# One product out of several in an adapter and feed-forward kernel: float32 replaced by float32r on operands split into exact parts

## The chip, the cores and the metric

The kernel runs on one core of a Trainium2 chip. The metric is the device time of one execution in microseconds (us). The core's engines appear in the profile as PE (TensorE, matrix products; PEld is its loading of weights), DVE (VectorE), ACT (ScalarE), POOL (GpSimd) and SP (the engine that here issues nearly all DMAs). A "q" behind a name (SPq) means the engine's sequencer. PSUM is the memory that PE writes; here it is eight buffers that all stages share.

## The reference

There are 8 batches of 256 tokens, x of shape (8, 256, 1024). Each batch b names one of 8 adapters by itok[b]. What is computed:

```
Bx  = x[b] @ B[id].T            # rank 16
c   = Bx @ A[id].T              # back to 1024
g   = fp8(c / in_scale) @ gate_w.T        # 2752 columns, weights are fp8 values
u   = fp8(c / in_scale) @ up_w.T
h   = silu(g * scales) * u * scales
out = x + (fp8(h / in_scale) @ down_w.T) * scales
```

The roundings to fp8 make it matter that c is as exact as float32: an error in c can move a value to its neighbour in fp8.

## The kernel before

The tokens are 2048 columns in four blocks t of 512 columns, two batches each. x is held transposed: 128 partitions by 8 slices k by 512 columns. The work goes in this order, and PE's order is the order of the program, since `multiply` (L470) pins every matmul to it.

- Block 0: `two_times_b(0)` (L500) forms Bx, `two_times_a(0)` (L531) forms c, and c is rounded to fp8 (xg) by `round_to` (L524), half on DVE (L527), half on ACT (L529). PE is kept busy by products of zeros ("warm", `pass_time`) until the data are there.
- `gate_up(c, 0)` (L581) for the first five chunks c of the hidden dimension (128 of 2752 columns each): 16 fp8 products of 512 columns into two PSUM buffers y (gate and up), then ACT's silu (g, L610) and DVE's product (hid, L611). In the fifth of them, twelve products in, `two_times_b(1)` is put between.
- Block 1: `two_times_a(1)`, then `gate_up(c, 1)` for the same five chunks. The first of these takes its slices of xg in turns of two, as they come. In the fourth, eight products in, `four_times_b()` (L552) forms Bx of the four batches of blocks 2 and 3; after it, `four_times_a` (L560) makes c for the first half of the 1024 rows, and in the middle of the fifth for the second half.
- Then `gate_up` of all other chunks and blocks, and the down projection (yd), each result with x added going out by DVE (o, L696) and SP.

The products with B and A are small and are packed by row or column quarters of PE's array. Each has float32 operands. For Bx, the 32 columns of B that a product takes (`b[:, at : at + 32]`) hold the 16 of one slice k and 16 of a neighbour or padding; the result is 32 rows in a quarter of PSUM's partitions. For block 1, A is stored in a zeroed tile so that only 16 of the quarter's 32 rows count (`load_a_two`, L370, row `32 * (2 * g + j) + R * j`); for blocks 2 and 3 only 16 rows of each quarter are used (L565). A group of c is four PSUM buffers, one for each row quarter q, and each buffer holds two slices k of 256 columns. In blocks 0 and 1 a product has 128 columns, because the two halves of Bx are placed in both orders (`other`) in the tile bm by copies of DVE and ACT (L517); in blocks 2 and 3 it has 256 columns, and bm is one copy of DVE (L557).

The loads stand on SP's queue in this order: x of block 0 with B and A of batches 0 and 1, the weights of the first five chunks, B of block 1 (two loads b), x of block 1 in two pieces (slices 0 to 6, 1792 KB; slice 7, 256 KB), A of block 1 (four loads of 32 KB), then x of block 2, two loads of b_four, x of block 3, two more, four loads of a_four (64 KB each), w_dt, and the weights of later chunks as their buffers come free. Each DMA of the queue waits for the semaphore of the DMA eight places before it.

The tiles hid0 to hid20 (128 by 2048 bytes) hold the rounded hidden values; chunk c writes hid[c], so most of them are empty in the first 60 us.

Of the kernel before, what the change touches and what calls it, by code (L numbers as in the profile page):

```python
# [8 lines left out]

F32 = mybir.dt.float32  # L10
BF16 = mybir.dt.bfloat16
FP8 = mybir.dt.float8e4
U16 = mybir.dt.uint16
I32 = mybir.dt.int32
AF = mybir.ActivationFunctionType
ALU = mybir.AluOpType
AX = mybir.AxisListType

P = 128
T = 2048  # L20
SEQ = 256
NB = 8
H = 1024
I = 2752
R = 16
NH = H // P
NI = (I + P - 1) // P
# [5 lines left out]
NFIRST = 5  # L33

BROW = NH * R + 8
# [15 lines left out]
def high(ap):  # L51

    return ap.bitcast(BF16)[..., 1::2]

# [229 lines left out]
def adaln_ffn(  # L284
# [13 lines left out]
    nc = tc.nc  # L298
    const = ctx.enter_context(tc.tile_pool(name="const", bufs=1))
# [22 lines left out]
    kept = ctx.enter_context(tc.tile_pool(name="kept", bufs=1))  # L322
    wpool = ctx.enter_context(tc.tile_pool(name="w", bufs=5))
    outs = ctx.enter_context(tc.tile_pool(name="outs", bufs=3))
    hid = [kept.tile([P, T], FP8, name=f"hid{c}") for c in range(NI - 1)]


    hid_tail = kept.tile([P, 2, TB], BF16, name="hid_tail")
# [8 lines left out]
    with ExitStack() as fast:  # L337
        acts = fast.enter_context(tc.tile_pool(name="acts", bufs=1))
        lora = fast.enter_context(tc.tile_pool(name="lora", bufs=1))
# [12 lines left out]
        b_two = [lora.tile([P, 2 * BROW + R], F32, name=f"b{t}") for t in range(2)]  # L352
        a_two = [lora.tile([P, H // 2], F32, name=f"a{t}") for t in range(2)]

        b_four = lora.tile([P, 4 * BROW + R], F32, name="b_four")
        a_four = lora.tile([P, H], F32, name="a_four")
        nc.gpsimd.memset(a_two[0], 0.0)
        nc.vector.memset(a_two[1], 0.0)
        for b, n in ((b_two[0], 2), (b_two[1], 2), (b_four, 4)):
            nc.vector.memset(b[:, n * BROW :], 0.0)  # L360

# [8 lines left out]
        def load_a_two(t, j, adapter, queue=nc.sync):  # L370
            for g in range(2):
                row = 32 * (2 * g + j) + R * j
                queue.dma_start(  # L373
                    out=a_two[t][row : row + R],
                    in_=a8[bass.ds(adapter * 2 * R + g * R, R), :],
                )

        def load_x(t, k):
            piece, first = x_of(x4, t, k)
            ks = slice(first, first + piece.shape[1])  # L380
            nc.sync.dma_start(out=xs[t][:, ks, :], in_=piece)
# [25 lines left out]
        adapters = [adapter_of(2 + q, nc.sync) for q in range(6)]  # L407
        for j in range(2):
            load_b(b_two[1], j, adapters[j], nc.sync)
        for k in (0, 7):  # L410
            load_x(1, k)
        for j in range(2):
            load_a_two(1, j, adapters.pop(0))

        for t in (2, 3):
            load_x(t, 0)
            for q in (2 * t - 4, 2 * t - 3):
                load_b(b_four, q, adapters[q], nc.sync)
        for q in range(4):
            nc.sync.dma_start(  # L420
                out=a_four[32 * q : 32 * q + R], in_=aT[bass.ds(adapters[q] * R, R), :]
            )


        sc = b_two[0][:, NH * R : BROW]
        inv = const.tile([P, 6], F32, name="inv")
# [43 lines left out]
        def multiply(*args, **kwargs):  # L470
            tc.keep_in_program_order(nc.tensor.matmul(*args, **kwargs))  # L471
# [12 lines left out]
        def times_b(bx, b, n, quads, between=None):  # L484


            for k in range(NH):
                for q, (i, row, t, cols) in enumerate(quads):
                    at = i * BROW + k * R - row
                    multiply(  # L490
                        bx[q][32 * q : 32 * (q + 1)],
                        lhsT=b[:, at : at + 32],
                        rhs=xs[t][:, k, cols],
                        start=(k == 0),
                        stop=(k == NH - 1),
                    )
                if between:
                    between(k)

        def two_times_b(t, between=None):  # L500


            n = SEQ // 2
            quads = [
                (j, R * j, t, slice(at, at + n))
                for half in range(2)
                for j in range(2)
                for at in (j * SEQ + half * n,)
            ]
            bx = [psum.tile([P, n], F32, tag="ps", name=f"bx{half}") for half in range(2)]  # L510
            times_b([bx[q // 2] for q in range(4)], b_two[t], n, quads, between)
            bm = lora.tile([P, 2, n], F32, tag="bm2", name="bm2", bufs=2)
            for other in range(2):
                for half, copy in enumerate((nc.vector.tensor_copy, nc.scalar.copy)):
                    to = half ^ other
                    tc.keep_in_program_order(
                        copy(  # L517
                            bm[64 * to : 64 * (to + 1), other],
                            bx[half][64 * half : 64 * (half + 1)],
                        )  # L520
                    )
            return bm

        def round_to(to, c, engine):  # L524
            scale = inv[:, GATE_IN : GATE_IN + 1]
# [2 lines left out]
            else:  # L528
                nc.scalar.activation(to, c, AF.Copy, scale=scale, saturate=False)  # L529

        def two_times_a(t, bm):  # L531


            n = SEQ // 2
            for part in range(2):
                cs = [psum.tile([P, 2, SEQ], F32, tag="ps", name=f"c{q}") for q in range(4)]
                for other, i in product(range(2), range(2)):
                    for q in range(4):
                        rows = slice(32 * q, 32 * (q + 1))
                        multiply(  # L540
                            cs[q][:, i, bass.ts(q // 2 ^ other, n)],
                            lhsT=a_two[t][rows, bass.ts(2 * part + i, P)],
                            rhs=bm[rows, other],
                            start=True,
                            stop=True,
                        )
                for q in range(4):
                    k = KS * part + 2 * (q // 2)
                    to = xg[t][:, k : k + 2, bass.ts(q % 2, SEQ)]
                    round_to(to, cs[q], nc.vector if q % 2 else nc.scalar)  # L550

        def four_times_b():  # L552
            quads = [(q, 0, 2 + q // 2, bass.ts(q % 2, SEQ)) for q in range(4)]
            bx = psum.tile([P, SEQ], F32, tag="ps", name="bx")
            times_b([bx] * 4, b_four, SEQ, quads)
            bm = lora.tile([P, SEQ], F32, tag="bm", name="bm", bufs=2)
            nc.vector.tensor_copy(bm, bx)  # L557
            return bm

        def four_times_a(bm, pairs):  # L560
            for i in pairs:
                cs = [psum.tile([P, 2, SEQ], F32, tag="ps", name=f"c{q}") for q in range(4)]
                for k in range(2):
                    for q in range(4):
                        rows = slice(32 * q, 32 * q + R)  # L565
                        multiply(
                            cs[q][:, k],
                            lhsT=a_four[rows, bass.ts(2 * i + k, P)],
                            rhs=bm[rows],
                            start=True,  # L570
                            stop=True,
                        )
                for q in range(4):
                    to = xg[2 + q // 2][:, 2 * i : 2 * i + 2, bass.ts(q % 2, SEQ)]
                    round_to(to, cs[q], nc.vector if q % 2 else nc.scalar)
# [5 lines left out]
        def gate_up(c, t, turns=(NH,), between=None):  # L581
# [4 lines left out]
            cols = bass.ts(t, TB)  # L586
# [6 lines left out]
            for i, (j, k) in enumerate(steps):  # L593
                if between and i == between[0]:
# [3 lines left out]
                    lhsT=high(w[:, k if tail else k // KS * NH + j * KS + k % KS, :]),  # L598
                    rhs=xg[t][:, k, :],
                    start=(k == 0),  # L600
                    stop=(k == NH - 1),
                )
            gates, ups = (ys[0], ys[-1]) if not tail else (ys[0][:TAIL], ys[0][TAIL:])
            rows = slice(TAIL, P) if tail else slice(0, P)
            if tail:
                to = lora.tile([P, 2 * TB], FP8, tag="bm", name="tail", bufs=2)[half_of(t), :TB]
            else:
                to = hid[c][:, cols]
            g = work.tile([P, TB], F32, tag="g", name="g")
            nc.scalar.activation(g[rows], gates, AF.Silu, scale=gate_s[: gates.shape[0]])  # L610
            nc.vector.scalar_tensor_tensor(  # L611
# [10 lines left out]
            if t == (NTB - 1 if c < NFIRST else 1):  # L622
                note_low_bits(w_of[c], P, c)
                if 1 < c <= 1 + 2 * NTB:
                    i, half = divmod(c - 2, 2)
# [9 lines left out]
        pass_time(warm, 16, TB)  # L635
        bm = two_times_b(0, lambda k: pass_time(warm, 4) if k == 6 else None)
        pass_time(warm, 7)
        two_times_a(0, bm)
        gate_up(0, 0, turns=(2, 2, 2, 2))
        for c in range(1, NFIRST - 1):  # L640
            gate_up(c, 0)
        bms = []
        gate_up(NFIRST - 1, 0, between=(12, lambda: bms.append(two_times_b(1))))
        two_times_a(1, bms[0])
        gate_up(0, 1, turns=(2, 2, 2, 2))
        for c in range(1, NFIRST - 2):
            gate_up(c, 1)
        gate_up(NFIRST - 2, 1, between=(8, lambda: bms.append(four_times_b())))
        four_times_a(bms[1], (0, 1))
        gate_up(NFIRST - 1, 1, between=(8, lambda: four_times_a(bms[1], (2, 3))))  # L650
        for c in range(NFIRST):
            for t in (2, 3):
                gate_up(c, t)
# [77 lines left out]
        for k in range(NH - 1):  # L731
# [24 lines left out]
            if first:  # L756
                tiles = down_tiles(NTB)
# [12 lines left out]
            if first:  # L770
# [5 lines left out]
                if not last:  # L776
                    tiles = down_tiles(NTB)
# [7 lines left out]
    with found_others.Else():  # L785

        k = NH - 1
        cut = TB - P
        tiles = down_tiles(NTB - 1)
# [7 lines left out]
        t, cols = NTB - 1, slice(cut, TB)  # L797
# [88 lines left out]
```

## Time and profile before

| What | us |
|---|---|
| median of 3 runs (475.91 to 476.14) | 475.91 |
| span of the profiled execution (first to last instruction) | 474.0 |
| median less span | 1.91 |
| PE busy in that span | 469.6 |
| ACT, DVE, POOL busy | 192.5, 105.6, 1.0 |
| c, block 1 (64 records of 128 columns) | 2.07 |
| c, blocks 2 and 3 (64 records of 256 columns, two calls) | 2.04 and 1.94 |

The page gives the span of the profiled execution and no other time of it. In the tables of the profile, a line has its start, its length, the engine, the line of the program, what is written from what, and in square brackets how long the engine had stood idle before it and what ended that. In the chain of waits a line has the start, the length and the work that the end hangs on in that time. A float32 product appears as two records: the 32 products with A of block 1 are 64 records.

### The profile page before, as it was taken

Reading aid. Unit: us, or ns where it says so; the run is one execution under the profiler, and the core shown is the slowest. Engines: PE = TensorE matmul, PEld = TensorE weight load, DVE = VectorE, ACT = ScalarE, POOL = GpSimd, SP = SyncE. Lnnn points to the kernel's source line nnn. Section 1 sums busy time; section 2 is a strip of 40 time slices with the busy share of each in tenths; the row PEclk is TensorE's granted clock in tenths of the full one; section 3 lists DMA queues with packets and bytes.
Section 4 is the critical chain, followed back from the end, with each engine's and each line's share of the span. In section 5 each row is a group of like instructions: output and inputs, shape, how many; then the busy total and the mean of one; then the engine's idle time right before and its main releaser. Section 6 shows DMA issues by size and latency. Waiting matters only on the chain.

```text
span 474.0 us, 6007 instructions
## 1 busy us (share of the span) xinstructions
PE 469.6 (99%) x2514; PEld 217.1 (46%) x2514; DVE 105.6 (22%) x163; ACT 192.5 (41%) x249; POOL 1.0 (0%) x7
## 2 busy tenths in 40 slices
PE   8999999999999999999999999999999999999997
PEld 5454544444444444444444444444444444444444
DVE  2332521212212121222212121232120121031031
ACT  2332438995555745443354544359212022021000
POOL 0000000000000000000000000000000000000000
DMA  8995023322222112222210121133335255163031
GB/s 316 416 406 153 1 90 115 153 89 90 89 89 90 54 45 80 90 89 89 90 57 36 41 62 56 61 100 106 115 135 162 66 184 160 28 212 110 3 116 67
DMA packets 13781, 53.45 MB, mean 113 GB/s; under 512 B 1650, under 2 KB 2930, under 8 KB 10802
## 3 DMA queue, kind: packets, MB, share of 16 engines
q1 hardware_dynamic: 13536, 52.86, 31.8%
q8 instruction: 21, 0.34, 0.3%
q10 hardware_dynamic: 210, 0.14, 0.1%
q14 instruction: 14, 0.11, 0.1%
HBM read 44.60 MB, written 8.39 MB: 112 GB/s over the span
## 4 chain that ended last, share of the span: by engine, by line
PE 96%; DMA 2%; ACTq 0%; ACT 0%; issue 0%; DVE 0%
PE y L471 62%; PE yd L471 32%; DMA w_gu<-w_gu 1%; PE c L471 1%; PE bx L471 1%; DMA a<-a 1%; ACT L307 0%; ACTq L373 0%; ACTq L306 0%; ACTq L366 0%; DVE o L696 0%; ACTq L363 0%; PE count L471 0%
## 5 line engine op out<-in xcount | busy, mean ns | idle before, releaser
L471 PE MATMUL y<-xg,w_gu 128*128 128x512 fp8e4 x1376 | 298.2, 379 | 0.1
L471 PEld LDWEIGHTS <-w_gu 128*128 128x128 bf16 x1376 | 134.1, 98 | 162.8 <-issue 1.3
L471 PE MATMUL yd<-hid,w_d 128*128 128x512 fp8e4 (+2 forms) x693 | 146.0, 373 | 0.0
L610 ACT ACTIVATE g<-y,gate_s 128x512 f32<-128x512 f32 (+1 forms) x88 | 59.8, 681 | 136.3 <-PE y L471 136.3
L611 DVE SCALAR_TENSOR_TENSOR hid<-y,up_by_down,g 128x512 fp8e4<-128x512 f32 x84 | 63.1, 751 | 219.4 <-PE y L471 161.6
L471 PEld LDWEIGHTS <-w_d 128*128 128x128 bf16 x693 | 66.6, 98 | 79.0 <-issue 1.7
L457 ACT ACTIVATE junk<-w_d 128x1408 bf16<-128x1408 uint16 (+1 forms) x16 | 21.2, 1324 | 88.5 <-DMA w_d<-w_d 88.4
L696 DVE SCALAR_TENSOR_TENSOR o<-yd,down_s,x 128x512 f32<-128x512 f32 x28 | 20.0, 748 | 107.3 <-PE yd L471 92.5
L457 ACT ACTIVATE junk<-w_gu 128x2048 bf16<-128x2048 uint16 (+1 forms) x22 | 41.0, 1863 | 0.0
L464 ACT ACTIVATE junk<-hid 128x2048 bf16<-128x2048 fp8e4 x21 | 40.0, 1904 | 0.4
L464 ACT ACTIVATE junk<-xg 128x2048 bf16<-128x2048 fp8e4 x8 | 15.3, 1909 | 0.3
L529 ACT ACTIVATE xg<-c,inv 128x512 fp8e4<-128x512 f32 x16 | 9.7, 688 | 8.6 <-PE c L471 8.6
L527 DVE TENSOR_SCALAR xg<-c,inv 128x512 fp8e4<-128x512 f32 x16 | 10.9, 745 | 2.8 <-PE c L471 2.8
L471 PE MATMUL warm<-zeros 128*128 128x512 bf16 (+1 forms) x27 | 6.6, 404 | 1.2 <-DVE zeros L309 1.2
L696 DVE SCALAR_TENSOR_TENSOR o<-yd,down_s,xg 128x512 f32<-128x512 f32 (+2 forms) x5 | 3.2, 644 | 12.3 <-PE yd L471 12.3
L517 ACT COPY bm<-bx 64x128 f32<-64x128 f32 x4 | 1.0, 262 | 9.2 <-PE bx L471 9.2
L471 PEld LDWEIGHTS <-zeros 128*128 128x128 bf16 x27 | 2.6, 117 | 4.8 <-issue 3.1
L471 PE MATMUL bx<-x,b 128*32 128x128 f32 x128 | 4.3, 276 | 0.1
L471 PE MATMUL c<-bm,a 32*128 32x128 f32 x128 | 4.3, 277 | 0.0
L457 ACT ACTIVATION_READ_ACCUMULATOR junk<-w_gu 128x1 f32 x22 | 4.2, 191 | 0.0
L471 PEld LDWEIGHTS c<-bm,a 32*128 32x128 f32 x128 | 3.9, 186 | 0.5 <-ACT bm L517 0.4
L471 PE MATMUL yd<-hid_tail,w_dt 64*128 64x512 bf16 (+1 forms) x32 | 4.1, 377 | 0.0
(47 smaller groups left out, 41.0 us busy)
## 6 DMA issues: line engine op xcount, KB each, us to landing
w_gu<-w_gu SPq DMA_DIRECT2D x20, 1024.0 KB, 4.8
outT<-o SPq DMA_DIRECT2D x31, 256.0 KB, 2.2
w_d<-w_d SPq DMA_DIRECT2D x8, 704.0 KB, 4.9
w_d<-w_d SPq DMA_DIRECT2D x8, 640.0 KB, 3.9
x<-x SPq DMA_DIRECT2D x2, 2048.0 KB, 11.3
x<-x SPq DMA_DIRECT2D x1, 1792.0 KB, 13.1
w_gu<-w_gu SPq DMA_DIRECT2D x3, 512.0 KB, 4.2
x<-x SPq DMA_DIRECT2D x2, 512.0 KB, 3.9
```

The costliest lines, as they stand in the source:

```text
L457: nc.scalar.activation(junk_like(w), low(w), AF.Copy, accum_out=lows[:rows, column : column + 1])
L464: nc.scalar.activation(junk_like(q), q, AF.Square, accum_out=squares[:rows, column : column + 1])
L471: tc.keep_in_program_order(nc.tensor.matmul(*args, **kwargs))
L517: copy(bm[64 * to : 64 * (to + 1), other], bx[half][64 * half : 64 * (half + 1)],)
L527: nc.vector.tensor_scalar(to, c, scale, None, ALU.mult, saturate=False)
L529: nc.scalar.activation(to, c, AF.Copy, scale=scale, saturate=False)
L610: nc.scalar.activation(g[rows], gates, AF.Silu, scale=gate_s[: gates.shape[0]])
L611: nc.vector.scalar_tensor_tensor(to, in0=ups, scalar=up_by_down[rows], in1=g[rows], op0=ALU.mult, op1=ALU.mult, saturate=False,)
L696: nc.vector.scalar_tensor_tensor(o, in0=y, scalar=down_s, in1=x, op0=ALU.mult, op1=ALU.add)
```

## The change

Blocks 1 to 3 form c with float32r operands. [...]

- Bx: `bm` is Bx rounded to float32r on the copy out of PSUM, and `rest` is the difference, by a subtraction on DVE. In block 1 the copies of bm are now one on DVE and three on ACT, with four subtractions on DVE; in blocks 2 and 3 one copy and one subtraction on DVE.
- A: each row quarter of A's tile holds the same 16 rows twice (`load_a_twice`), so there are 8 loads of 32 KB for block 1 and 8 of 64 KB for blocks 2 and 3, twice as many as before. A tile `minus` of -1 in the upper half of each quarter and 0 in the lower half is made by an iota on POOL and two small operations on DVE. On POOL, `parts = a * minus` rounded to float32r and `parts = a + parts` then leave the rounded part in one half and the remainder in the other.
- B: copies on POOL (`twice`) place the same 16 columns twice side by side, so that Bx stands in both halves of each quarter.
- c is then two products in one PSUM group, A's parts with bm and A's parts with rest, each over 32 rows: 64 multiplications for block 1 and 64 for blocks 2 and 3, where there were 32 and 32.
- The last slice of x of block 1 is loaded behind A's eight loads instead of ahead of four.
- The new tiles lie in buffers of hid9 to hid20 until those are written. The memset of block 1's A on DVE goes. Block 0 stays as it was.

In the built program POOL's iota follows a reload of POOL's library; the two DVE operations for `minus` stand ahead of block 0's copies of bm on DVE; and the four subtractions of block 1 stand ahead of DVE's product for hid of chunk 4.

The diff, cut to its core:

```diff
-        nc.vector.memset(a_two[1], 0.0)
...
+        def load_a_twice(a, q, src, at):
+            for row in (32 * q, 32 * q + R):
+                nc.sync.dma_start(out=a[row : row + R], in_=src[bass.ds(at, R), :])
...
-        for k in (0, 7):
-            load_x(1, k)
+        load_x(1, 0)
         for j in range(2):
-            load_a_two(1, j, adapters.pop(0))
+            adapter = adapters.pop(0)
+            for g in range(2):
+                load_a_twice(a_two[1], 2 * g + j, a8, adapter * 2 * R + g * R)
+        load_x(1, 7)
...
         for q in range(4):
-            nc.sync.dma_start(
-                out=a_four[32 * q : 32 * q + R], in_=aT[bass.ds(adapters[q] * R, R), :]
-            )
+            load_a_twice(a_four, q, aT, adapters[q] * R)
+        lane = const.tile([P, 1], I32, name="lane")
+        nc.gpsimd.iota(lane, pattern=[[0, 1]], base=0, channel_multiplier=1)
+        nc.vector.tensor_scalar(lane, lane, R, None, ALU.bitwise_and)
+        minus = const.tile([P, 1], F32, name="minus")
+        nc.vector.tensor_scalar(minus, lane, -1.0 / R, None, ALU.mult)
+
+        def two_parts_of(a, slot, name, cuts=1):
+            parts = in_place_of_hid(slot, list(a.shape), F32R, name)
+            n = a.shape[1] // cuts
+            for cols in (bass.ts(i, n) for i in range(cuts)):
+                nc.gpsimd.tensor_scalar(
+                    parts[:, cols], a[:, cols], minus, None, ALU.mult
+                )
+                nc.gpsimd.tensor_tensor(
+                    parts[:, cols], a[:, cols], parts[:, cols].bitcast(F32), ALU.add
+                )
+            return parts
+
+        def twice(b, n, name, slot):
+            tiles = []
+            for i in range(n):
+                to = in_place_of_hid(slot - i, [P, NH, 2, R], F32, f"{name}{i}")
+                row = b[:, i * BROW : i * BROW + NH * R].rearrange("p (k r) -> p k r", r=R)
+                for copy in range(2):
+                    nc.gpsimd.tensor_copy(to[:, :, copy], row)
+                tiles.append(to.rearrange("p k c r -> p (k c r)"))
+            return lambda i, k, row: tiles[i][:, 2 * R * k : 2 * R * (k + 1)]
+
+        b_twice = [twice(b_two[1], 2, "b_twice", NI - 2)]
+        a_parts = [two_parts_of(a_two[1], NI - 8, "a_parts", cuts=2)]
+        b_twice.append(twice(b_four, 4, "b_four_twice", NI - 4))
+        for i in range(2):
+            a = a_four[:, bass.ts(i, H // 2)]
+            a_parts.append(two_parts_of(a, NI - 9 - i, f"a_four_parts{i}"))
...
             for other in range(2):
                 for half, copy in enumerate((nc.vector.tensor_copy, nc.scalar.copy)):
                     to = half ^ other
-                    tc.keep_in_program_order(
+                    if t and other:
+                        copy = nc.scalar.copy
+                    held(
                         copy(
                             bm[64 * to : 64 * (to + 1), other],
                             bx[half][64 * half : 64 * (half + 1)],
                         )
                     )
+                for half in range(2 if t else 0):
+                    to = half ^ other
+                    rows = slice(64 * half, 64 * (half + 1))
+                    held(
+                        nc.vector.tensor_tensor(
+                            rest[64 * to : 64 * (to + 1), other],
+                            bx[half][rows],
+                            bm[rows, 0].bitcast(F32),
+                            ALU.subtract,
+                        )
+                    )
...
-                for other, i in product(range(2), range(2)):
+                for other, i, bm in product(range(2), range(2), bms):
                     for q in range(4):
                         rows = slice(32 * q, 32 * (q + 1))
                         multiply(
                             cs[q][:, i, bass.ts(q // 2 ^ other, n)],
-                            lhsT=a_two[t][rows, bass.ts(2 * part + i, P)],
+                            lhsT=a[rows, bass.ts(2 * part + i, P)],
                             rhs=bm[rows, other],
-                            start=True,
-                            stop=True,
+                            start=bm is bms[0],
+                            stop=bm is bms[-1],
                         )
...
             nc.vector.tensor_copy(bm, bx)
-            return bm
+            rest = in_place_of_hid(NI - 13, [P, SEQ], F32R, "rest4")
+            nc.vector.tensor_tensor(rest, bx, bm.bitcast(F32), ALU.subtract)
+            return bm, rest
...
                 for k in range(2):
-                    for q in range(4):
-                        rows = slice(32 * q, 32 * q + R)
-                        multiply(
-                            cs[q][:, k],
-                            lhsT=a_four[rows, bass.ts(2 * i + k, P)],
-                            rhs=bm[rows],
-                            start=True,
-                            stop=True,
-                        )
+                    for bm in bms:
+                        for q in range(4):
+                            rows = slice(32 * q, 32 * (q + 1))
+                            multiply(
+                                cs[q][:, k],
+                                lhsT=a[i // 2][rows, bass.ts(2 * (i % 2) + k, P)],
+                                rhs=bm[rows],
+                                start=bm is bms[0],
+                                stop=bm is bms[-1],
+                            )
```

More of the change, by code (lines that the diff above doesn't have):

```diff
@@ L11 @@
 BF16 = mybir.dt.bfloat16
+F32R = mybir.dt.float32r
 FP8 = mybir.dt.float8e4
@@ L324, in adaln_ffn, with hid_of, in_place_of_hid @@
     outs = ctx.enter_context(tc.tile_pool(name="outs", bufs=3))
-    hid = [kept.tile([P, T], FP8, name=f"hid{c}") for c in range(NI - 1)]
+    hid = {}
+    def hid_of(c):
+        if c not in hid:
+            hid[c] = kept.tile([P, T], FP8, tag=f"hid{c}", name=f"hid{c}")
+        return hid[c]
+    def in_place_of_hid(c, shape, dtype, name):
+        return kept.tile(shape, dtype, tag=f"hid{c}", name=name)
     hid_tail = kept.tile([P, 2, TB], BF16, name="hid_tail")
@@ L488, in times_b @@
                 for q, (i, row, t, cols) in enumerate(quads):
-                    at = i * BROW + k * R - row
                     multiply(
                         bx[q][32 * q : 32 * (q + 1)],
-                        lhsT=b[:, at : at + 32],
+                        lhsT=b(i, k, row),
                         rhs=xs[t][:, k, cols],
@@ L504, in two_times_b @@
             quads = [
-                (j, R * j, t, slice(at, at + n))
+                (j, 0 if t else R * j, t, slice(at, at + n))
                 for half in range(2)
@@ L510, in two_times_b, with as_loaded @@
             bx = [psum.tile([P, n], F32, tag="ps", name=f"bx{half}") for half in range(2)]
-            times_b([bx[q // 2] for q in range(4)], b_two[t], n, quads, between)
-            bm = lora.tile([P, 2, n], F32, tag="bm2", name="bm2", bufs=2)
+            def as_loaded(i, k, row):
+                at = i * BROW + k * R - row
+                return b_two[t][:, at : at + 32]
+            b = b_twice[0] if t else as_loaded
+            times_b([bx[q // 2] for q in range(4)], b, n, quads, between)
+            bm = lora.tile([P, 2, n], F32R if t else F32, name=f"bm{t}")
+            if t:
+                rest = in_place_of_hid(NI - 11, [P, 2, n], F32R, "rest")
+            held = tc.keep_in_program_order
             for other in range(2):
@@ L521, in two_times_b @@
                     )
-            return bm
+                for half in range(2 if t else 0):
[9 more added lines that the diff above has]
+                    )
+            return (bm, rest) if t else (bm,)
         def round_to(to, c, engine):
@@ L529, in round_to, with two_times_a @@
                 nc.scalar.activation(to, c, AF.Copy, scale=scale, saturate=False)
-        def two_times_a(t, bm):
+        def two_times_a(t, bms, a):
             n = SEQ // 2
@@ L554, in four_times_b, with four_times_a @@
             bx = psum.tile([P, SEQ], F32, tag="ps", name="bx")
-            times_b([bx] * 4, b_four, SEQ, quads)
-            bm = lora.tile([P, SEQ], F32, tag="bm", name="bm", bufs=2)
+            times_b([bx] * 4, b_twice[1], SEQ, quads)
+            bm = in_place_of_hid(NI - 12, [P, SEQ], F32R, "bm4")
             nc.vector.tensor_copy(bm, bx)
-            return bm
-        def four_times_a(bm, pairs):
+            rest = in_place_of_hid(NI - 13, [P, SEQ], F32R, "rest4")
+            nc.vector.tensor_tensor(rest, bx, bm.bitcast(F32), ALU.subtract)
+            return bm, rest
+        def four_times_a(bms, pairs, a):
             for i in pairs:
@@ L607, in gate_up @@
             else:
-                to = hid[c][:, cols]
+                to = hid_of(c)[:, cols]
             g = work.tile([P, TB], F32, tag="g", name="g")
@@ L637, in adaln_ffn @@
         pass_time(warm, 7)
-        two_times_a(0, bm)
+        two_times_a(0, bm, a_two[0])
         gate_up(0, 0, turns=(2, 2, 2, 2))
@@ L643, in adaln_ffn @@
         gate_up(NFIRST - 1, 0, between=(12, lambda: bms.append(two_times_b(1))))
-        two_times_a(1, bms[0])
+        two_times_a(1, bms[0], a_parts[0])
         gate_up(0, 1, turns=(2, 2, 2, 2))
@@ L648, in adaln_ffn @@
         gate_up(NFIRST - 2, 1, between=(8, lambda: bms.append(four_times_b())))
-        four_times_a(bms[1], (0, 1))
-        gate_up(NFIRST - 1, 1, between=(8, lambda: four_times_a(bms[1], (2, 3))))
+        four_times_a(bms[1], (0, 1), a_parts[1:])
+        gate_up(NFIRST - 1, 1, between=(8, lambda: four_times_a(bms[1], (2, 3), a_parts[1:])))
         for c in range(NFIRST):
```

## The prediction

> **What bounds the kernel now.** I read the page first, then the chain of waits in order of time, then the timelines around the three blocks, then SP's own queue.
>
> ```profile
> span 474.0 us, 6007 instructions
> ...
> PE 469.6 (99%) x2514; PEld 217.1 (46%) x2514; DVE 105.6 (22%) x163; ACT 192.5 (41%) x249; POOL 1.0 (0%) x7
> ...
> PE 96%; DMA 2%; ACTq 0%; ACT 0%; issue 0%; DVE 0%
> ```
>
> TensorE (PE) is the end: 96% of the chain is its own work and the engine stands idle almost nowhere. A microsecond taken out of its stream, or a microsecond for which it is made to wait, moves the end by a microsecond. The chain in order of time shows the part that the change touches:
>
> ```profile
> 28.95 1.88 PE bx L471 x64
> 30.84 0.97 PE y L471 x4
> 31.81 2.07 PE c L471 x64
> 33.87 12.19 PE y L471 x56
> 46.07 3.59 PE bx L471 x64
> 49.66 1.83 PE y L471 x8
> 51.49 2.04 PE c L471 x32
> 53.53 1.83 PE y L471 x8
> 55.37 1.94 PE c L471 x32
> 57.30 264.29 PE y L471 x1224
> ```
>
> The first four lines are block 1, the next six are blocks 2 and 3. Only the three lines "c" get a new kind of product: 2.07 + 2.04 + 1.94 = 6.05 us in all. VectorE (DVE) beside them, from the timeline of each stage:
>
> ```profile
> 30.87 0.60 DVE L517 COPY bm<-bx 64x128 f32<-64x128 f32 x2 [3.65 <-PE bx L471]
> ...
> 31.91 0.75 DVE L611 SCALAR_TENSOR_TENSOR hid<-y,up_by_down,g 128x512 fp8e4<-128x512 f32 x1 [0.45 <-PE y L471]
> ...
> 32.97 2.73 DVE L527 TENSOR_SCALAR xg<-c,inv 128x512 fp8e4<-128x512 f32 x4 [0.31 <-PE c L471]
> ```
>
> ```profile
> 51.60 0.75 DVE L611 SCALAR_TENSOR_TENSOR hid<-y,up_by_down,g 128x512 fp8e4<-128x512 f32 x1 [1.45 <-PE y L471]
> ...
> 52.63 2.73 DVE L527 TENSOR_SCALAR xg<-c,inv 128x512 fp8e4<-128x512 f32 x4 [0.28 <-PE c L471]
> ...
> 56.50 2.73 DVE L527 TENSOR_SCALAR xg<-c,inv 128x512 fp8e4<-128x512 f32 x4 [1.15 <-PE c L471]
> ```
>
> The evictions follow the products closely, with gaps of 0.3 to 1.2 us only: DVE has little room. And SP's queue:
>
> ```profile
> 15.10 0.90 SPq L381 DMA_DIRECT2D x<-x  x2
> 16.27 7.21 SPq L373 DMA_DIRECT2D a<-a  x4
> ...
> 24.14 4.42 SPq L366 DMA_DIRECT2D b_four<-b  x2
> ```
>
> The two x loads of block 1 (1792 and 256 KB) are issued at 15.1 and 15.5, long before use. The built order gives each DMA a wait for the one eight places before it; the second b_four issue stood 3.6 us for that reason, until the 1792 KB of x landed at 28.2.
>
> **The change part by part.**
>
> *The products themselves.* A float32 product stands in the trace as two records. Four of them, one in each row quarter, run together: block 1 does 16 quartets of 128 columns in 2.07 us (0.129 each), blocks 2 and 3 do 16 quartets of 256 columns in 3.98 (0.25 each), so about 0.12 us for each further 128 columns, 0.93 ns a column. y's fp8 products take 264.29/1224 = 0.216 us for 512 columns, 0.42 ns a column. The trace shows no float32r. Its cheap end is one record at y's rate (256 columns: 0.11 us), its dear end two records like float32. After, there are twice as many products, 64 for block 1 and 64 for blocks 2 and 3, so 16 quartets each at one record. Blocks 2 and 3 would take 16 x 0.11 = 1.8 us at one end and 2 x 3.98 = 8.0 at the other, 3.98 if one record keeps float32's rate. [...] That is 2.1 us, **1.9 less**. Block 1 would take 16 x (0.06 to 0.13) = 1.0 to 2.07 us.
>
> *What is late next in blocks 2 and 3.* The eight PSUM buffers. The built order lets the fourth c of the second group wait for DVE. That is L611, which reads the y just finished, from 51.60 to 52.35. Before, the second group began at 52.5 and met nothing; now the first is done at 51.49 + 4 x 0.13 = 52.0, so PE stands until 52.4 and ends the call at 52.4 + 0.45 = 52.85 instead of 53.53. The next call starts at 54.68, its second group could start at 55.2, but its last buffer is that of the gate y (ScalarE L610, 0.7 us from 54.8): 55.55, end 56.0 instead of 57.30. **Gain 1.3** of the 1.9. [...] The extra DVE subtraction (about 0.43, as the copy at L557) lies under the 1.83 us of eight y products.
>
> *Block 1: DVE.* One copy goes to ScalarE, four subtractions come: five DVE operations of 0.30 instead of two, ahead of L611 and of the first eviction. Copy from 30.87: 5 x 0.30 = 32.37, L611 to 33.09, eviction to 33.83, y at 33.9 against 33.81 to 33.87 now. So whatever the 128-column products save below 0.129 is lost to DVE, and **0.1 is added**.
>
> *Block 1: the loads.* A's loads become eight of 32 KB, and all stand before the 256 KB of x. The eighth A waits for the 1792 KB (28.2), is issued for 0.34, and only then x's last slice, at 28.65. Alone in the queue it takes between 2.2 us (the 256 KB stores of outT) and 3.0 (the line through the lone weight loads: 640 KB in 3.9, 1024 KB in 4.8). It lands at 30.85 to 31.65. The eighth k of bx wants it at 28.95 + 7/8 x 1.88 = 30.6. **PE waits 0.25 to 1.05 us; I take 0.9**, nearer to the loads, as it is one.
>
> *Block 1: GpSimd.* A's parts can begin when the eighth A has landed, 28.24 + 2.4 = 30.65. Two multiplications and one addition of 256 columns must be over for the first c, at 32.7 after that wait. POOL's only wide row is a memset (512 columns, 0.53). One input at its rate is 0.3, two inputs at twice that: 0.3 + 0.3 + 0.6 = 1.2, ready at 31.9, hidden. At three times that price c would start 1.5 us later; below, nothing is to be won. b_twice (four copies of 128 columns after b landed at 23.6, before 28.9) and the four-batch work (b copies after x lands near 41, bx at 46; eight a_four DMAs landing near 44, about 3.5 us of POOL, c at 51.5) have 3 to 5 us of cover.
>
> *Start.* DVE's two operations for the lane mask wait for POOL's iota, ahead of which the built program reloads POOL's library. Behind them on DVE stand block 0's bm copies, at 9.59. POOL is free at 1.55. The nearest rows are ScalarE's table load (1.28 us) and the slowest load in this stage (w_gu, 11.0): iota over between 2.9 and 12.6, and with 0.4 for the two operations a cost of 0 to 3.4 us. I take 0. [...]
>
> *At nothing:* the memset of a_two[1] (0.49 at 1.28, DVE then idle to 6.29); SP's eight added issues (w_gu's next issue waits 30 us for PE anyway); hid's buffers lent out (hid9 and later are written after 100 us).
>
> **Sum.** -1.3 + 0.1 + 0.9 = -0.3 us on the profiled span of 474.0. The page gives no other time of that execution; the median of the runs, 475.91, is 1.91 above the span, and I leave that as it is: **475.6**. A measurement here can tell about 0.2% (0.95 us) from no change, so this is "the same".
>
> **Rivals.** (1) *The slice of x lands like a store and the buffers come free early.* -1.9 + 0.1 + 0.25 = -1.55: 474.4. For it: outT's 2.2; against: DVE's small gaps, and loads are slower. Chance 0.18. (2) *Slower: float32r streams at float32's rate*, that is, the change doesn't halve anything, in place "c". One record at 0.93 ns a column: no gain in blocks 2 and 3, block 1 keeps its 1.0: 476.9; if only the 128-column products are dear (two records, 4.1 us instead of 2.07), c ends block 1 at 32.7 + 4.1 = 36.8 instead of 34.9, 1.9 more than forecast: 477.5; dear everywhere, 4.0 more again on top of the lost 1.3: 482.8. It decides from a 256-column quartet above 0.15 on, where 1.3 has sunk to 1.0. For it: float32 rows are the only 4-byte rows, and all stream at 0.93. Chance 0.23. (3) *POOL's reload holds DVE in block 0.* It costs from an iota end at 9.2 on, one for one, but swallows the 0.9 wait for x, which is set by the DMA queue; at the dear end 3.4 + 0.1 - 1.3 = +2.2: 478.1. Chance 0.12. The forecast has 0.47, with 474.8 to 476.8 as its own range.
>
> **Range.** 474.4 takes in rival 1; 478.2 takes in rival 3 and rival 2 without the case of dear products everywhere: some 0.85 lies within. Faster by over 0.2% (below 474.96): most of rival 1 and an edge of the forecast, 0.20. Slower (above 476.86): most of rivals 2 and 3 and an edge, 0.33. Within: 0.47.
>
> **What will show it.** c's quartets of 256 columns: 0.13 right, 0.25 or more rival 2. PE idle before the last bx of block 1, released by DMA x, about 0.9. A stall inside each half of blocks 2 and 3, released by DVE or ACT. y of block 1 released by xg L527. POOL's iota before 9.2. I am wrong by much if float32r needs two records, if POOL's additions take over 1.5 us, or if PE's pause makes the granted clock, 1.00 throughout now, fall.

## The result, and the profile after

The changed kernel takes 477.34 us (median of 20 runs, 476.34 to 480.59), the kernel before 476.06 us (20 runs, 475.69 to 477.07). The ratio is 1.0034, with a 95% interval of 1.0022 to 1.0045: slower by 1.1 to 2.1 us. The prediction said 475.6 us, 0.3 less than before; the time lies in its range, on the wrong side. All ratios here and below lie near the ratio of the means, so single long runs weigh in them: of the 31 runs of the kernel before with a median of 475.89, four took 478.3 to 479.1, and there the difference of the medians is the steadier number.

The span of the profiled execution went from 474.0 to 475.4 us. The page of the changed kernel:

```profile
span 475.4 us, 6064 instructions
...
PE 92%; DMA 4%; SPq 1%; DVE 1%; issue 0%; ACTq 0%; ACT 0%; DVEq 0%
```

PE's share of the chain fell from 96% to 92%, and DMA's rose from 2% to 4%: something now waits for a load. The chain in order of time says where (start, length, work):

```profile
28.85 3.27 DMA x<-x
...
32.16 0.44 PE bx L526 x8
...
34.22 0.76 DVE hid L690
...
35.03 1.10 PE c L526 x28
36.13 12.19 PE y L526 x56
...
53.86 0.76 DVE hid L690
...
54.66 0.74 PE c L526 x12
55.40 1.83 PE y L526 x8
57.23 1.51 PE c L526 x30
58.74 264.29 PE y L526 x1224
```

Two places can be set against the lines of before. Block 1's first y starts at 36.13 instead of 33.87: **2.26 us lost**. From there to the y that ends blocks 2 and 3 it is 22.61 us (58.74 - 36.13) instead of 23.43 (57.30 - 33.87): **0.82 us won**. The sum, +1.44, is the whole change of the span. The y of block 2 after that and everything behind it take as long as before.

What precedes the loss stands in SP's queue:

```profile
15.99 12.81 SPq L390 DMA_DIRECT2D a<-a  x8
28.85 0.90 SPq L395 DMA_DIRECT2D x<-x  x2
```

The eight loads of A take SP from 16.0 to 28.8, since the eighth waits for x's first piece (landed at 28.49). Only then x's last slice goes out. It lands 3.27 us later, and PE, which wanted it at 30.6, stands still for 1.55 us:

```profile
28.87 1.74 PE L526 MATMUL bx<-x,b_twice 128*32 128x128 f32 x56
...
32.16 0.42 PE L526 MATMUL bx<-x,b_twice 128*32 128x128 f32 x8 [1.55 <-DMA x<-x]
```

The new products and GpSimd's parts, from the timelines of block 1 and of blocks 2 and 3:

```profile
30.61 1.83 POOL L453 TENSOR_SCALAR a_parts<-a,minus 128x256 fp32r<-128x256 f32 x2 [6.14 <-DMA a<-a]
...
32.40 1.40 POOL L456 TENSOR_TENSOR a_parts<-a,a_parts 128x256 fp32r<-128x256 f32 x2
...
33.76 0.28 PE L526 MATMUL c<-bm,a_parts 32*128 32x128 f32 x4
...
33.87 0.28 PE L526 MATMUL c<-rest,a_parts 32*128 32x128 f32 x4
```

```profile
54.02 0.29 PE L526 MATMUL c<-bm,a_four_parts 32*128 32x256 f32 x4
...
54.14 0.29 PE L526 MATMUL c<-rest,a_four_parts 32*128 32x256 f32 x4
```

Each of these PE lines is a quartet of records, and the starts are what counts: 0.11 us apart with 128 columns, 0.12 with 256. Float32 had taken 0.129 and 0.25 a quartet, and the number of records is the same (64 and 64). So with float32r the products with A take half their time at 256 columns, and hardly less at 128.

### The profile page after: what moved, and what is told of

Same layout as the page of the kernel before. It is cut to its first block, busy times and chain, and to the rows that moved or that the text cites. A ratio compares the mean times of both kernels' runs of the same rounds, so it can differ in the third digit from the quotient of the medians.

```text
span 475.4 us, 6064 instructions
## 1 busy us (share of the span) xinstructions
PE 469.1 (99%) x2514; PEld 216.5 (46%) x2514; DVE 106.4 (22%) x168; ACT 192.7 (41%) x250; POOL 12.9 (3%) x28
## 4 chain that ended last, share of the span: by engine, by line
PE 92%; DMA 4%; SPq 1%; DVE 1%; issue 0%; ACTq 0%; ACT 0%; DVEq 0%
PE y L526 59%; PE yd L526 31%; DMA x<-x 3%; DMA a<-a 1%; PE bx L526 1%; PE c L526 1%; SPq L373 1%; SPq L405 0%; DVE hid L690 0%; DVE rest L591 0%; SPq L376 0%; ACT L308 0%; ACTq L383 0%; ACTq L307 0%; ACTq L376 0%
## 5 line engine op out<-in xcount | busy, mean ns | idle before, releaser
L690 DVE SCALAR_TENSOR_TENSOR hid<-y,up_by_down,g 128x512 fp8e4<-128x512 f32 x84 | 63.1, 751 | 218.6 <-PE y L526 159.7
L690 DVE SCALAR_TENSOR_TENSOR tail<-y,up_by_down,g 64x512 fp8e4<-64x512 f32 x4 | 3.0, 756 | 4.9 <-ACT g L689 4.8
L519 ACT ACTIVATION_READ_ACCUMULATOR junk<-hid 128x1 f32 x21 | 3.9, 187 | 0.0
L526 PE MATMUL bx<-x,b_twice 128*32 128x128 f32 x64 | 2.2, 276 | 1.6 <-DMA x<-x 1.6
L526 PE MATMUL bx<-x,b_four_twice 128*32 128x256 f32 x64 | 3.7, 380 | 0.0
```

The lines of the kernel that those rows point to most:

```text
L519: nc.scalar.activation(junk_like(q), q, AF.Square, accum_out=squares[:rows, column : column + 1])
L690: nc.vector.scalar_tensor_tensor(to, in0=ups, scalar=up_by_down[rows], in1=g[rows], op0=ALU.mult, op1=ALU.mult, saturate=False,)
```

## The experiments

My theory after the result: all of the loss is in block 1 and comes from the place and number of A's loads (x waits, then GpSimd and DVE are late); blocks 2 and 3 gain, less than the products alone would give because PSUM buffers come free late. Rivals: float32r with its subtractions and parts costs wherever it stands; or the wait for x is the whole loss. All ratios are to the kernel before, with the 95% interval; the median beside them is the run's.

**Blocks 2 and 3 alone.** Block 1 as before the change:

```diff
-        load_x(1, 0)
-        for j in range(2):
...
-                load_a_twice(a_two[1], 2 * g + j, a8, adapter * 2 * R + g * R)
-        load_x(1, 7)
+        for k in (0, 7):
+            load_x(1, k)
+        for j in range(2):
+            load_a_two(1, j, adapters.pop(0))
...
-        two_times_a(1, bms[0], a_parts[0])
+        two_times_a(1, bms[0], a_two[1])
```

> Block 1 as before the change (float32, four loads of A behind both pieces of x), blocks 2 and 3 as after it. My theory now: the whole loss sits in block 1, where PE waits 1.55 us for the last slice of x and then 0.70 more for GpSimd's parts and DVE's queue, and blocks 2 and 3 gain 0.8 us (11.24 us from bx to the first y of block 2 before, 10.42 after). Then 476.06 - 0.8 = 475.25 us, and the spread of the runs shrinks to that of the kernel before. Rival: the extra work on GpSimd and DVE costs wherever it stands, and block 1's loads only took the blame; then 476.5 or more.

Measured: 475.35 us (475.09 to 475.86) against 475.89, ratio 0.9982 (0.9971 to 0.9994). As the theory has it; the rival's 476.5 is out.

**Block 1 alone.** Blocks 2 and 3 as before the change:

```diff
-            load_a_twice(a_four, q, aT, adapters[q] * R)
+            nc.sync.dma_start(
+                out=a_four[32 * q : 32 * q + R], in_=aT[bass.ds(adapters[q] * R, R), :]
+            )
...
-        four_times_a(bms[1], (0, 1), a_parts[1:])
+        four_times_a(bms[1], (0, 1))
```

> Block 1 as after the change, blocks 2 and 3 as before it (float32). My theory: +2.25 us, 478.3, with the wide spread of the changed kernel, since the wait for x's last slice is in it. Rival as in the run with blocks 2 and 3 alone: less than the changed kernel, below 477.3.

Measured: 478.12 us, ratio 1.0036 (1.0016 to 1.0055). In its chain x's slice again goes out late, at 29.04, and takes 2.88 us, and block 1's y starts at 35.93. The two halves of the change are +2.2 and -0.5 by the medians, together +1.7; the whole had +1.3 by its medians and 1.1 to 2.1 by its interval, so they agree within the scatter.

**x's last slice ahead of A's loads.** The changed kernel with one move undone:

```diff
-        load_x(1, 0)
+        for k in (0, 7):
+            load_x(1, k)
...
-        load_x(1, 7)
```

> The changed kernel with x's last slice loaded ahead of A's eight loads, as it stood before the change; nothing else. My theory: the wait for x (1.55 us) goes, but the eighth load of A then waits for that slice, is issued at about 29.1 and lands near 31.8, and GpSimd needs 2.8 us from there to the first usable part; c of block 1 starts near 34.6 instead of 33.5 and y near 36.5 instead of 36.1: 477.7, no better. Rival: the wait for x is the whole of the loss, so 477.3 - 1.5 = 475.8.

Measured: 478.9 us, ratio 1.0056 (1.0037 to 1.0076). The rival falls: PE no longer waits for x (bx runs through in 1.95 us), but waits 1.96 us for GpSimd's first part, since A's eighth load now waits for x's slice and goes out only at 29.9:

```profile
32.10 1.83 POOL L453 TENSOR_SCALAR a_parts<-a,minus 128x256 fp32r<-128x256 f32 x2 [6.91 <-DVE bm L581]
...
34.68 0.33 PE L526 MATMUL c<-bm,a_parts 32*128 32x128 f32 x4 [1.96 <-POOL a_parts L456]
```

The trace puts GpSimd's start down to DVE's copy of bm, which ended in that moment. A's eighth load is the likelier cause: its issue ends at 30.2, and in the changed kernel GpSimd starts 1.8 us after the end of that issue (30.61 against 28.81), which is 32.0 too; in the next run, with the same loads, GpSimd starts before bm's copy ends (31.16 against 31.21) and the trace names the load.

The run is also 1.2 us worse than I had expected. The windows of its profile show why (time, then busy time and number of instructions of each engine, granted clock, DMA share):

```profile
core 0: us, PE busy (x) PEld busy (x) DVE busy (x) ACT busy (x) POOL busy (x), PEclk, DMA share, GB/s
...
32.00:34.00 2.00, 0.72 (x4) 0.10 (x2) 1.82 (x6) 0.62 (x3) 1.90 (x3) 1.00 0.76 303
...
36.00:38.00 2.00, 2.00 (x32) 1.06 (x25) 2.00 (x4) 2.00 (x4) 0.00 (x0) 0.74 0.93 372
38.00:40.00 2.00, 2.00 (x6) 0.76 (x5) 0.58 (x1) 0.24 (x1) 1.00 (x4) 0.50 1.11 467
40.00:42.00 2.00, 2.00 (x10) 0.84 (x8) 0.00 (x0) 0.36 (x1) 0.00 (x0) 0.91 0.99 418
42.00:44.00 2.00, 2.00 (x11) 0.91 (x10) 0.75 (x1) 0.53 (x2) 0.00 (x0) 1.00 0.93 250
```

After the pause of 32.7 to 34.7 the granted clock falls to 0.74 and 0.50, and is back at 1.00 from 42 us on. The number of products in a window tells the price: 6 in 2 us instead of 11.

**The pause filled.** The same with products of zeros in it:

```diff
+        filler = psum.tile([P, TB], F32, tag="ps", name="filler")
+        pass_time(filler, 9, TB)
         two_times_a(1, bms[0], a_parts[0])
```

> The run with x's last slice ahead of A's loads, with nine products of zeros of 512 columns (0.216 us each, 1.95 us) put on PE between the last y of chunk 4 and c of block 1, where PE stood still for 1.96 us. They add work that nothing uses. My theory: the 1.2 us by which that run was above what I had expected are the granted clock, which fell to 0.50 to 0.9 of full speed from 36 to 42 us after the pause; with PE busy it stays at 1.00 and the time is 477.7. Rival: the clock's fall is a symptom without a price, or the extra comes from loads; then 478.9 as without the filling, or more.

Measured: 476.99 us (476.8 to 477.68), ratio 1.0026 (1.0016 to 1.0035). The clock is 1.00 in every window from 28 to 42 us, with the same loads in flight:

```profile
31.16 1.83 POOL L453 TENSOR_SCALAR a_parts<-a,minus 128x256 fp32r<-128x256 f32 x2 [6.70 <-DMA a<-a]
```

```profile
36.00:38.00 2.00, 2.00 (x11) 0.93 (x10) 1.65 (x3) 1.30 (x3) 0.41 (x2) 1.00 1.11 444
38.00:40.00 2.00, 2.00 (x11) 0.88 (x9) 0.26 (x1) 0.69 (x1) 0.59 (x3) 1.00 0.98 410
```

It is faster by 1.9 us for doing more: the pause, not the loads, brought the clock down. From the first c, behind the pause, to the end the two profiles take 443.0 and 441.4 us, so the clock's fall cost about 1.7. The runs say the same: with x's slice first, seven of eight had a mean clock of 0.996 or 0.993, and the one at 1.00 took 477.59; with the pause filled all eleven were at 0.999 or more. The two profiled executions are 2.6 us apart (479.47 and 476.85) because in the first bx also starts 0.84 later (29.79 against 28.95), ahead of what the edit touches. The time is 0.7 below my 477.7, since I had A's eighth load landing at 31.8 and c at 34.6; GpSimd starts at 31.16 and c at 33.74.

**A loaded early by GpSimd.**

```diff
-                nc.sync.dma_start(out=a[row : row + R], in_=src[bass.ds(at, R), :])
+                queue.dma_start(out=a[row : row + R], in_=src[bass.ds(at, R), :])
...
         load_a_two(0, 1, second, nc.sync)
+        for j in range(2):
+            adapter = adapter_of(2 + j, nc.gpsimd)
+            for g in range(2):
+                load_a_twice(a_two[1], 2 * g + j, a8, adapter * 2 * R + g * R, nc.gpsimd)
```

> The changed kernel, with block 1's eight loads of A issued by GpSimd's own DMA queue at the start instead of by SP's queue, and x's last slice back right behind x's first; the products stay as changed. My theory: the place of these loads is the cost. Without it PE waits neither for x nor for GpSimd in block 1. What stays is DVE's longer queue and the second group's fourth PSUM buffer, which waits for hid of chunk 4: from the end of bx to the first y the changed kernel takes 0.5 us more than the kernel before. So before + 0.5 - 0.8 = 475.6 to 475.8. Rival: block 1's float32r products, their subtractions and GpSimd's parts cost as such; then not below 477.

Measured: 477.72 us, ratio 1.0039 (1.0026 to 1.0053). My expectation was missed by 2 us, and by itself the number would speak for the rival. The trace says otherwise. From the start of the kernel, and then from block 1:

```profile
17.60 0.61 PE L527 MATMUL y<-xg,w_gu 128*128 128x512 fp8e4 x2 [0.99 <-DMA w_gu<-w_gu]
```

```profile
35.06 0.33 PE L527 MATMUL c<-rest,a_parts 32*128 32x128 f32 x4 [0.77 <-DVE rest L592]
```

Neither x nor GpSimd is waited for in block 1. But the eight small loads ran beside the first weights, and the second chunk of these came at 17.60 instead of 15.8, so bx starts 1.78 us late (30.66). And the order that the build chose put DVE's product for hid between the subtractions, so that c waits 0.77 for `rest`. The wait was moved, not removed; the run does not separate theory and rival.

**A's rows stored twice.** The same loads without their number: each quarter's 32 rows lie together in memory and come with one DMA; x's slice stays behind A; DVE's order in block 1 is pinned to that of the changed kernel.

```diff
-            for row in (32 * q, 32 * q + R):
-                nc.sync.dma_start(out=a[row : row + R], in_=src[bass.ds(at, R), :])
+            nc.sync.dma_start(
+                out=a[32 * q : 32 * q + 2 * R], in_=src[bass.ds(2 * at, 2 * R), :]
+            )
...
+        "aT2": np.tile(np.asarray(L0_cond_A).transpose(0, 2, 1), (1, 2, 1)).reshape(2 * P, H),
...
-        "a8": a8.reshape(8 * 2 * R, H // 2),
+        "a8": np.tile(a8, (1, 1, 2, 1, 1)).reshape(8 * 4 * R, H // 2),
```

> The changed kernel, with A stored twice in a row in memory, so that each quarter's 32 rows come with one DMA: four loads of 64 KB for block 1 and four of 128 KB for blocks 2 and 3 in place of eight and eight; same order on SP's queue, x's last slice behind A. DVE's order in block 1 is pinned to that of the changed kernel. My theory: the loss is the wait of the eighth load, and of x behind it, for x's first piece. With four loads, x's last slice waits only for the weights' last chunk (landed at about 23) and lands right behind the rest, near 29; A's last load lands near 28.8, GpSimd's first part is ready near 31.6, and PE waits for neither. Block 1 then costs 0.4 to 0.5 us more than before the change (DVE's queue and the PSUM buffer behind it), blocks 2 and 3 gain 0.8: 475.5 to 475.7. Rival: float32r with its subtractions and GpSimd parts costs in block 1 as such, as the run with A loaded early (477.7) could also be read; then not below 476.5.

Measured: 475.69 us against 475.83, ratio 1.0000 (0.9991 to 1.0009). PE's lines of block 1:

```profile
28.95 1.95 PE L528 MATMUL bx<-x,b_twice 128*32 128x128 f32 x64
...
32.50 0.33 PE L528 MATMUL c<-bm,a_parts 32*128 32x128 f32 x4 [0.62 <-POOL a_parts L458]
...
34.48 5.79 PE L528 MATMUL y<-xg,w_gu 128*128 128x512 fp8e4 x26
```

bx runs through; c waits 0.62 us for GpSimd (A landed at 29.7, not at 28.8), y starts 0.67 later than before the change. Same products, same bytes, same subtractions and parts, four loads instead of eight: 1.65 us less than the changed kernel, or 1.4 when each median is set against that of the kernel before beside it. So most of block 1's loss comes with the loads, and the rival, which had not below 476.5, is out. What it says holds for the 0.67 that stays: that is GpSimd's parts, with DVE's queue close behind. In this trace hid ends at 33.29; with the 1.10 us that followed it in the changed kernel, y would start at 34.4 instead of 34.48 even if GpSimd were on time (an estimate).

**The groups of c spread.** Blocks 2 and 3 alone, as in the first run, with the four groups placed one by one:

```diff
-        four_times_a(bms[1], (0, 1), a_parts[1:])
-        gate_up(NFIRST - 1, 1, between=(8, lambda: four_times_a(bms[1], (2, 3), a_parts[1:])))
+        pair(0)
+        gate_up(
+            NFIRST - 1, 1, between={6: lambda: pair(1), 10: lambda: pair(2), 14: lambda: pair(3)}
+        )
```

Here `pair(i)` is `four_times_a(bms[1], (i,), a_parts[1:])`.

> As the run with blocks 2 and 3 alone, and the four groups of c of blocks 2 and 3 put one by one: the first where it was, the others after 6, 10 and 14 of the 16 products of chunk 4, instead of two by two. My theory: what blocks 2 and 3 gain is cut by waits for PSUM buffers (each call's fourth buffer, 0.9 us after the call's start). Spread, c costs 16 quartets of 0.115 us = 1.85 instead of 3.98, so 2.0 us less than before the change: 474.0. [...] Second rival: the waits move along and nothing more is won: 475.25.

Measured: 475.03 us (474.8 to 475.66), ratio 0.9974 (0.9960 to 0.9988). It beats both kernels, but by 1.0 less than I had expected. The chain of this kernel:

```profile
51.55 0.68 PE c L524 x16
52.23 1.40 PE y L524 x6
53.63 0.67 PE c L524 x15
```

No group waits for a buffer any more, and still one takes 0.68 us where four quartets of 0.117 make 0.47. From y to c and back PE loses 0.21, four times, 0.84 in all. My expectation had left that out.

**Both together, and once more without block 1.** A's rows stored twice with the groups spread, and the spread kernel again beside it.

> As the run with A's rows stored twice, and the four groups of c of blocks 2 and 3 one by one. My theory: 0.3 less than that run, 475.2 to 475.4, above the spread kernel with block 1 in float32 beside it, since block 1 cannot gain behind DVE. Rival: with its loads right, block 1 in float32r gains too; then below the spread kernel's 475.0.

> The spread kernel with block 1 in float32 once more, on the chip of the two runs beside it, for a direct comparison. My theory: 475.0, the fastest of the three. Rival: slower than the run with A's rows stored twice and the groups spread.

Measured: 475.38 us, ratio 0.9992 (0.9983 to 1.0001), and 475.01 us, ratio 0.9984 (0.9975 to 0.9993). Block 1 in float32r does not pay with four loads either: by the medians it costs 0.37, and in the run with A's rows stored twice c waits 0.62 us for GpSimd. With GpSimd on time it would still be late by the estimate above; no run had it so. Spreading on top of the early loads by GpSimd gave 477.32, ratio 1.0033 (1.0020 to 1.0045), 1.8 to 2.0 above what I had expected, for the reasons told there (the first weights' second chunk came at 17.41, and hid again stands between the subtractions); it is 0.4 below the run without spreading:

> As the run with A loaded by GpSimd's queue, and the four groups of c of blocks 2 and 3 put one by one as in the earlier run. My theory: 0.3 less than without the spreading, 475.3 to 475.5, so 0.3 to 0.5 above the spread kernel that leaves block 1 in float32 (475.03): 128-column products in float32r gain almost nothing, because a quartet takes 0.113 us in them against 0.129. Rival: block 1 in float32r pays once its loads are early; then below 475.0.

## Why the prediction went wrong

- *What bounds the kernel:* right. Each microsecond of PE's stand in block 1 came back at the end: 2.26 lost there and 0.82 won behind it make 1.44, and the span grew from 474.0 to 475.4.
- *The products:* right. One record each, at 0.117 us a quartet of 256 columns, so rival 2 (float32's rate) fell. The forecast's 2.1 us for blocks 2 and 3 are 16 quartets at 0.13, near the 0.129 of block 1 in float32; no run shows the 0.13 or why one record should do at that price, and 0.117 is what was measured in its place.
- *"What is late next in blocks 2 and 3 ... Gain 1.3":* the mechanism was right, the size not. The fourth buffer waits for hid L690 and then for ACT's g, 0.98 and 0.85 us after each call's start, as worked out (0.91 and 0.87). But from there I took 0.45 to the end, and it is 0.67 and 0.66: the change from one kind of product to the other (0.21 there and back in the spread kernel) was not priced. Gain 0.82.
- *"PE waits 0.25 to 1.05 us; I take 0.9":* this is the step that failed most. The mechanism was the forecast one, but the wait was 1.55, above its upper end: x's first piece was issued 0.25 later than in the profile of before (15.35 against 15.10) and landed 0.28 later, and the slice took 3.27 instead of at most 3.0 (2.88 in the run with block 1 alone). I had put the upper end at a line through two other loads, and left the landing time of x's first piece without any scatter. To the wait comes 0.2 us, since the last bx, once alone, takes 0.44 instead of 0.235: 1.75 where the sum has 0.9. I had also priced the slice as alone in its queue; but 2 MB of x for block 2 are issued right behind it (both issues lie between 28.85 and 29.75). Whether that made it slower no run shows. Rival 1, with 2.2 us for the slice, fell with it.
- *"0.1 is added" (DVE in block 1):* 0.5. I had the order of DVE right (its sum is off by 0.03: 32.37 + 0.75 is 33.12, not 33.09), but let y wait for the first eviction after L611 only. In fact the fourth buffer of the second group waits for the same L611 (now L690), as in blocks 2 and 3: from 35.03, when it is free, seven more quartets and 1.10 us to y.
- *GpSimd:* no cost, but by luck. Two multiplications took 1.83 us and the first addition 0.7, 2.5 instead of 1.2. From 30.61 that is 33.1, and with the forecast wait c would have wanted the part at 32.7. It was hidden by the longer wait for x; in the run with x's slice first, it was the bound.
- *Start:* rival 3 fell. The iota began at 1.57 us, 0.04 behind POOL's memset of a (1.01 to 1.53), and took 0.13; the forecast had it over between 2.9 and 12.6.
- *The sum:* -1.3 + 0.1 + 0.9 was to be -0.3; measured, -0.82 + 0.5 + 1.75 = +1.43. Three terms, two with the right mechanism and DVE's with the wrong last wait, were each off to the same side. With terms of opposite sign and 1 us each, the sign of the sum was not to be had from a central value; the chance of 0.2 for "faster" and 0.33 for "slower" said so better than the forecast did. The last sign of being wrong, a fall of the granted clock in PE's pause, did not show in the changed kernel's profile, but in the run with x's slice first.

That block 1 could be left in float32 at no loss could have been read beforehand: its 128-column quartets at 0.129 us had four weight loads in them, and these do not shrink (0.18 us each, four side by side, in both kernels). It is a reading that fits the numbers (0.113 and 0.117 for 128 and 256 columns in float32r); no run took the weight loads away.

## What to carry to other kernels

Count DMAs, not bytes, when a load is doubled: on a queue where each waits for the one eight places before it, four more small loads put a late load behind an early large one (here x's 256 KB went out at 28.85, once the 1792 KB had landed at 28.49, and PE stood for 1.55 us). Before splitting products, look at whether more columns take more time: here float32 took twice as long for 256 columns as for 128 (0.25 and 0.129 us a quartet) and gained by half (0.117), while 128 columns gained almost nothing (0.113). That the weight loads set the pace there is the reading above, not shown. And where a change's terms cancel, undo its halves one at a time on the chip: here one half was worth keeping (475.35, with the groups spread 475.0) and the other not.

## What the runs showed of the hardware

- *A pause cost the clock.* With x's slice first, a stand of PE of 1.96 us was followed, some 2.3 us after its end, by about 3.4 us at a granted clock of 0.50 (an estimate, 37.0 to 40.4 us: the means of the windows above, 0.74, 0.50 and 0.91, with the clock taken as 1.00 on either side); products of zeros in the pause kept it at 1.00 in every window from 28 to 42 us. The pause of 1.55 us in the changed kernel's profile left the clock at 1.00. Its two longest runs (480.19 and 480.59 us) had a mean clock of 0.993, but the run with block 1 alone, where x's slice again comes late (landed at 31.92), had no such run in eleven, and three of 31 runs of the kernel before were at 0.996 without that pause. What brought the clock down in these single runs stays open.
- *GpSimd's one-input operation was dearer than its two-input one:* 0.93 us for 256 columns with a scalar per partition, 0.72 for the addition; 1.56 and 1.27 for 512. Both round to float32r; the profile's spans on GpSimd are rough.
- *A load issued when nothing else moved:* in the changed kernel, at 28.5 to 28.9 us, 32 KB landed 1.7 us after its issue, and 256 KB, with 2 MB issued behind it, 3.3 us.
